# A four-layer conditioned transformer on one core: modulations computed with the condition as weights, and an MLP that may start before the last attention block ends

## The chip, the core and the metric

The kernel runs on one core of a Trainium2 chip. The core has five engines that work at the same time, each through its own list of instructions in order: TensorE (PE in the profile) multiplies matrices, VectorE (DVE), ScalarE (ACT) and GpSimd (POOL) work on elements, and SyncE (SP) here only issues DMAs. Engines wait for one another through semaphores. The metric is the time of one execution on the device, in microseconds.

## The reference

The input `x` has 16 samples of 256 tokens and 256 features. It passes through four layers, L0 to L3, and all of it is in 32-bit floats. L0, L2 and L3 have self-attention (16 heads of 16 features), cross-attention to a context of 77 tokens, and an MLP of width 1024. L1 has cross-attention alone. The layers' norms are shifted and scaled by vectors that come from the condition, one vector per sample:

```python
# L2; L0 and L1 are alike, and L3 takes c without the silu
c_proj = jax.nn.silu(c) @ W_mod + b_mod          # c is 16 x 256
shift_a, scale_a, gate_a, shift_m, scale_m, gate_m = jnp.split(c_proj, 6, axis=-1)
x_norm = modulate(_ln(x), shift_a, scale_a)      # t * (1 + sc[:, None]) + shift[:, None]
...
x_norm2 = modulate(_ln(x), shift_m, scale_m)
h = jax.nn.gelu(x_norm2 @ W_mlp1 + b_mlp1)
h = h @ W_mlp2 + b_mlp2
x = x + gate_m[:, None] * h
```

Ten such pairs of shift and scale are needed in the four layers. (L0 takes its condition without the silu too.) Attention uses an exponential for its softmax, the MLP a gelu; both are functions that ACT looks up in tables.

## The kernel before

**Blocks.** `x` stays in on-chip memory for the whole run (`x_sb`). The work is cut into blocks, one for each sample and each attention or MLP. `attention` (line 729 on) makes one attention block, `mlp` (line 1037 on) one MLP block. The stages follow each other as a, b (L0), c, d (L1 and L2), e, f (L3): a, c and e are attention, b, d and f are MLP. Within an attention stage the blocks of all samples are mixed, self-attention of one sample beside cross-attention of another.

**The planner.** The program's order is not that of the code. Each block adds tasks to a list (`od.add`): an engine, an assumed duration, the function that issues the instructions, the tasks it depends on, the buffers it takes, and a priority that grows from block to block. `Order.solve` then plays the list through with these durations. Whenever an engine is free it takes, of the tasks whose dependences and buffers are there, the one with the lowest priority (on TensorE), and two tasks that use different 32-row parts of TensorE's array are started as a pair (`rp`). The tasks are issued in the order that comes out, and every engine keeps to it on the chip, so an engine whose next instruction waits holds back all that stands behind it. A change in one assumed duration can move tasks anywhere after it. A pool of buffers is named by its tag; `b` are the eight PSUM banks that TensorE writes to, `kq` five large buffers that hold queries and keys, or weights, and `tmp` two buffers.

**One attention block.** A norm (DVE statistics at L460 and L461, POOL reciprocal root at L466 and L467, POOL scaling at L491) is turned by DVE (L519) and two DMAs (L524 out, L528 in), and ACT applies the modulation (L539). TensorE multiplies with the weights (L619, in 32-column parts; L628), in rotated blocks the result goes by DVE and POOL (L704) and is turned back by TensorE (L724). TensorE's scores for the maxima (L844, L856) go to DVE (L874, L878); the scores for the softmax (L937) to ACT's exponential (L949, L951); TensorE multiplies with the values (L960); DVE and POOL divide (L969, L976, L982, L986); `residual` multiplies with the output weights (L619 again) and adds to `x_sb`.

**One MLP block.** The same norm, then four tasks of TensorE with the first weights (L1059), each followed by a pair of gelus on ACT (L1064), then the second weights (L1010, in two halves). The weights (1 MB each) lie in two `kq` buffers.

**Barriers.** The task lists hold two kinds of wait between stages. `before` (all norms of the attention stage are done) holds the MLP's norms. `barrier` (all exponentials of the attention stage are done) holds the MLP's first product: `open_h` at line 1049 has it among its dependences, and nothing of L1059 can start before it. In the other direction, `attention` has a barrier of its own at its exponentials, which waits for all gelus of the MLP stage before. The gates' rows that an MLP block loads (`gate_tasks`) wait for `barrier` too.

**A modulation.** `modulation` (line 368 on) loads 512 columns of the weights (256 features by 512 columns, two rows of tiles `k`), and multiplies. The weights are TensorE's stationary side (`lhsT`), the condition, 16 columns, its moving side, so that the result stands with features on partitions, as ACT needs it at L539. These are eight multiplications at L382. DVE adds the bias (L387) and the 1 of the scale. The rows for the gates are computed the other way round, with the condition as the stationary side (L411). The modulations of L1 to L3 are placed beside MLP blocks of the stage before (`when`).

Of the kernel before, what the change touches and what calls it, by code (L numbers as in the profile page):

```python
# [58 lines left out]


class Task:
    __slots__ = ("eng", "dur", "run", "deps", "take", "prio", "rp", "left", "ready", "outs", "held", "start", "end", "no", "since", "kind", "more",
                 "lat", "first", "mb")


# [8 lines left out]
class Order:  # L74
# [3 lines left out]
    TURN = {"row": 0.2, "col": 0.13}  # L78
    PATIENCE = 2.0
    FAVOUR = 3.0  # L80
    PER_MB = 2.7
    def __init__(self, caps):
        self.caps, self.tasks = caps, []
# [14 lines left out]
        self.tasks.append(t)  # L98
        return t

    def solve(self):
        import heapq
        caps = self.caps
        loose = {k: list(range(n)) for k, n in caps.items()}
        free, waiting, events, result = {}, {}, [], []
        seq, n_done, now, mode, moved = 0, 0, 0.0, None, 0.0
        for t in self.tasks:
            if not t.left:
                waiting.setdefault(t.eng, []).append(t)

        def room(t, more=()):
            need = {}
            for h in list(t.take) + list(more):
                if h.no < 0:
                    need[h.tag] = need.get(h.tag, 0) + 1
            return all(len(loose[k]) >= n for k, n in need.items())

        def begin(ts):
            nonlocal seq, mode, moved
            dur = max(t.dur for t in ts) + sum(t.more for t in ts)  # L120
            if ts[0].eng == "PE":
                kind = "row" if ts[0].rp is not None else ts[0].kind
                dur += self.TURN.get(kind, 0.2) if kind != mode else 0.0
                mode = kind
            for t in ts:
                for h in t.take:
                    if h.no < 0:
                        h.no = loose[h.tag].pop(0)
                t.start, t.end = now, now + dur + t.lat
                if t.mb:  # L130
                    moved = max(now + dur, moved) + t.mb * self.PER_MB
                    t.end = moved + t.lat
                waiting[t.eng].remove(t)
                seq += 1
                heapq.heappush(events, (t.end, seq, t))
            if ts[0].eng != "NO":
                free[ts[0].eng] = now + dur
            result.append((now, len(result), ts))

        def choose(cand):  # L140

            lone = None
            for t in cand:
                if t.rp is None:
                    return [t]
                mates = [u for u in cand if u.rp == 1 - t.rp and room(t, u.take)]
                if mates:
                    return [t, min(mates, key=lambda u: (u.kind == t.kind, u.prio, u.no))]
                if lone is None:
                    lone = t  # L150
                    if t.since is None:
                        t.since = now
            if lone is not None and (now >= lone.since + self.PATIENCE - 1e-9 or not events):
                return [lone]
            return None

        while n_done < len(self.tasks):
            progress = True
            while progress:
                progress = False  # L160
                for eng in list(waiting):
                    if eng != "NO" and free.get(eng, 0.0) > now + 1e-9:
                        continue
                    cand = [t for t in waiting[eng] if t.ready <= now + 1e-9]
                    cand.sort(key=lambda t: (t.prio, t.no) if eng == "PE" else (not t.first, t.prio, t.no) if eng in ("SP", "NO") else
                              (not t.first, t.ready - self.FAVOUR * any(h.tag == "b" for h in t.held), t.prio, t.no))
                    cand = [t for t in cand if room(t)]
                    if cand:
                        ts = choose(cand) if eng == "PE" else [cand[0]]
                        if ts is not None:  # L170
                            begin(ts)
                            progress = True
            nxt = [e[0] for e in events[:1]]
            nxt += [t.ready for ts in waiting.values() for t in ts if t.ready > now + 1e-9]
            nxt += [t.since + self.PATIENCE for t in waiting.get("PE", ())
                    if t.since is not None and t.since + self.PATIENCE > now + 1e-9]
            assert nxt, "no step can start"
            now = min(nxt)
            while events and events[0][0] <= now + 1e-9:
                _, _, t = heapq.heappop(events)  # L180
                n_done += 1
# [13 lines left out]
def pixart_kernel(ctx: ExitStack, tc: tile.TileContext, x, cond_t, ctx_in, mask_c, mask_s, tables, vecs, rows,  # L195
# [32 lines left out]
    def psum(h, *dims):  # L228

        t = banks[h.no]  # L230
        return t.rearrange("p (a b) -> p a b", a=dims[0]) if dims else t
# [134 lines left out]
    gate_d, gate_t = {}, {}  # L366

    def modulation(name, src, col, shift_at, scale_at, c_t, bias, norm=None, gate=None, deps=(), prio=0, gprio=None):
        hw, hm, s = Hold("kq"), Hold("b"), {}
        m = mods[name] = const.tile([P, 4, B], F32, name=f"mod_{name}")  # L370

        def load():
# [1 line left out]
            nc.sync.dma_start(s["w"], src[:, :, col:col + 512])  # L374

        def mults():
            ps = psum(hm)
            s["ps"] = ps[:, 0:4 * B].rearrange("p (s b) -> p s b", b=B)
            for i, at in enumerate((shift_at, scale_at)):
                for c in range(NC):  # L380
                    for k in range(NC):
                        nc.tensor.matmul(s["ps"][:, 2 * i + c, :], lhsT=s["w"][:, k, at + c * P:at + (c + 1) * P],  # L382
                                         rhs=c_t[:, k, :], start=(k == 0), stop=(k == NC - 1))

        def take():
            v = vec[:, VOFF[bias]:VOFF[bias] + 4].unsqueeze(2).to_broadcast([P, 4, B])
# [4 lines left out]
                for c in range(NC):  # L391
                    nc.vector.tensor_scalar(m[:, 2 + c, :], m[:, 2 + c, :], 1.0, vcol(norm, c), ALU.add, ALU.mult)
        t0 = add("SP", ISSUE, load, deps=deps, take=[hw], prio=prio, mb=0.5, lat=2.0)
        t1 = add("PE", 2.0, mults, deps=[t0], take=[hm], use=[hw], prio=prio)
        mod_t[name] = add("DVE", 0.6, take, deps=[t1], use=[hm], prio=prio)
        if gate is None:
            return
# [639 lines left out]
    def mlp(b, name, wv, h_w, w_t, eps, mod, func, b1, pre_add, gate, prio, barrier, before):  # L1037
        s, nm = {}, f"{name}{b}"
        x_t = join([x_done[b], before], prio)
        xT_t, hx = norm_tasks(s, b, eps, mod, nm, prio, deps=[x_t])  # L1040
        if gate is not None:
            gate_tasks(s, b, gate, nm, prio, [barrier, xT_t])
        early_add(s, b, pre_add, prio)
        gel, he = [], Hold("ec")

        def open_h():
            for i in range(4):
                s["h", i] = buf(he)[:, i]
        t_h = add("NO", 0.0, open_h, deps=[xT_t, w_t["w1"], barrier], take=[he], prio=prio)
        for i in range(4):  # L1050
            hq, u = Hold("b"), {}

            def mm(i=i, u=u, hq=hq):
                ps = psum(hq)
                u["p"] = ps.rearrange("p (j n) -> p j n", j=2)
                for j in range(2):
                    f = 2 * i + j
                    for k in range(NC):
                        nc.tensor.matmul(u["p"][:, j, :], lhsT=wv["w1"][:, k, f * P:(f + 1) * P],  # L1059
                                         rhs=s["xT"][:, k, :], start=(k == 0), stop=(k == NC - 1))  # L1060

            def act(i=i, u=u):
                for j in range(2):
                    nc.scalar.activation(s["h", i][:, j, :], u["p"][:, j, :], func, bias=vcol(b1, 2 * i + j))  # L1064
            a = add("PE", 4 * MM, mm, deps=[t_h], take=[hq], use=[he, hx, *h_w], prio=prio)
            gel.append(add("ACT", 0.98, act, deps=[a], use=[hq, he], prio=prio))
        residual(s, b, [*gel, w_t["w2"]], lambda k, t: s["h", k // 2][:, k % 2, t * P:(t + 1) * P], lambda: wv["w2"], NF,
                 [he, *h_w], gate, nm, prio)
        return gel
# [311 lines left out]
```

## Time and profile before

Three runs took 2614.37, 2617.77 and 2619.29 us. A fourth execution was profiled.

| What | Value |
|---|---|
| Median of three runs | 2617.77 us |
| The profiled execution's own time | 2619.31 us |
| Its span, first instruction to last | 2617.4 us |
| Mean granted TensorE clock | 0.991 of full speed |
| TensorE instructions with L382 (modulations) | 160, in 21.4 us |
| ACT busy | 1284.3 us in 2559 instructions |
| ACT table loads | 6, of 1283 ns each |
| First gelu of the stages b, d, f | at 631.5, 1595.9, 2393.5 us |

A line such as `L382` is a line of the kernel. A multiplication in 32-bit floats stands in the trace as two instructions, a turn by TensorE as one. The waits name the engine that waited, the operation it waited for, the total in us, how often, and the longest. The granted clock is the share of TensorE's full clock; at half of it a matmul takes twice its time, and the profile still calls TensorE busy.

### The profile page before, as it was taken

Reading aid. Unit: us, or ns where it says so; the run is one execution under the profiler, and the core shown is the slowest. Engines: PE = TensorE matmul, PEld = TensorE weight load, DVE = VectorE, ACT = ScalarE, POOL = GpSimd, SP = SyncE. Lnnn points to the kernel's source line nnn. Section 1 sums busy time; section 2 is a strip of 40 time slices with the busy share of each in tenths; the row PEclk is TensorE's granted clock in tenths of the full one; section 3 lists DMA queues with packets and bytes.
Section 4 is the critical chain, followed back from the end, with each engine's and each line's share of the span. In section 5 each row is a group of like instructions: output and inputs, shape, how many; then the busy total and the mean of one; then the engine's idle time right before and its main releaser. Section 6 shows DMA issues by size and latency. Waiting matters only on the chain. (4 is left out here: it accounts for less than half of the span.)

```text
span 2617.4 us, 71563 instructions
## 1 busy us (share of the span) xinstructions
PE 2562.5 (98%) x29192; PEld 1677.9 (64%) x29192; DVE 1596.0 (61%) x4489; ACT 1284.3 (49%) x2559; POOL 1138.9 (44%) x1429
## 2 busy tenths in 40 slices
PE   8999999999999899999999999999999999998999
PEld 4555555556888656555556567888555555566888
DVE  6788886775130567777777784111878887885100
ACT  2555555564333456565556564232455555554322
POOL 5344434566552355333335566432233334557310
PEclk9999999999999899999999999999999999999999
DMA  5110111224221121111111123111100001121110
GB/s 173 31 32 26 35 33 40 69 79 136 69 78 53 40 70 51 57 52 40 40 41 46 55 79 106 60 61 41 36 28 28 28 28 38 46 77 57 57 57 29
DMA packets 159809, 144.08 MB, mean 55 GB/s; under 512 B 24648, under 2 KB 124216, under 8 KB 158712
## 3 DMA queue, kind: packets, MB, share of 16 engines
q1 hardware_dynamic: 159480, 139.51, 17.1%
q8 instruction: 229, 3.75, 0.6%
q14 instruction: 100, 0.82, 0.1%
HBM read 91.86 MB, written 47.61 MB: 53 GB/s over the span
## 5 line engine op out<-in xcount | busy, mean ns | idle before, releaser
L951 ACT ACTIVATE ec<-bank 128x512 f32<-128x512 f32 (+1 forms) x1152 | 611.6, 596 | 505.1 <-PE bank L844 300.2
L937 PE MATMUL bank<-kq 32*128 32x256 f32 (+1 forms) x5120 | 638.3, 395 | 4.9 <-ACT ec L949 2.7
L491 POOL TENSOR_SCALAR xn<-x_sb,mv,rstd 128x256 f32<-128x256 f32 x320 | 452.6, 1469 | 112.4 <-DVE y L519 101.3
L937 PEld LDWEIGHTS bank<-kq 32*128 32x128 f32 (+1 forms) x5120 | 360.3, 167 | 186.5 <-issue 96.7
L844 PE MATMUL bank<-kq 32*128 32x512 f32 x1536 | 446.8, 634 | 1.6 <-ACT ec L951 0.8
L874 DVE TENSOR_REDUCE mx<-bank 128x2 f32<-128x512 f32 x544 | 342.3, 680 | 59.3 <-PE bank L844 58.2
L1064 ACT ACTIVATE ec<-bank,vec 128x256 f32<-128x256 f32 x384 | 159.9, 467 | 403.1 <-PE bank L1059 365.5
L960 PE MATMUL bank<-ec,v 128*32 128x256 f32 (+1 forms) x5120 | 351.7, 385 | 5.2 <-ACT ec L951 2.9
L1059 PE MATMUL bank<-xT,kq 128*128 128x256 f32 x1536 | 344.1, 381 | 0.0
L1010 PE MATMUL bank<-kq,ec 128*128 128x256 f32 x1536 | 340.2, 379 | 0.0
L1059 PEld LDWEIGHTS bank<-xT,kq 128*128 128x128 f32 x1536 | 291.9, 191 | 42.1 <-issue 2.8
L1010 PEld LDWEIGHTS bank<-kq,ec 128*128 128x128 f32 x1536 | 291.2, 190 | 41.3 <-issue 2.1
L982 POOL TENSOR_TENSOR od<-ts,rec 128x128 f32<-128x128 f32 x448 | 170.9, 403 | 319.5 <-DVE rec L976 319.3
L519 DVE STREAM_TRANSPOSE y<-xn 128x512 f32<-128x512 f32 x158 | 110.6, 700 | 306.9 <-DMA yd<-y 255.2
L960 PEld LDWEIGHTS bank<-ec,v 128*32 128x32 f32 (+1 forms) x5120 | 156.4, 110 | 158.6 <-issue 39.4
L878 DVE TENSOR_REDUCE mx<-bank 128x4 f32<-128x308 f32 x512 | 211.6, 468 | 41.5 <-PE bank L937 30.0
L870 DVE CUSTOM_DVE_ANT_0 junk<-bank,ctx 128x256 f32<-128x256 f32 x448 | 189.0, 422 | 51.6 <-PE bank L844 22.1
L969 DVE STREAM_TRANSPOSE ts<-bank 128x512 f32<-128x512 f32 x224 | 157.8, 705 | 68.0 <-PE bank L960 57.9
L466 POOL TENSOR_SCALAR rstd<-mv 128x2 f32<-128x2 f32 x160 | 37.9, 237 | 352.8 <-DVE mv L461 281.3
L704 POOL TENSOR_TENSOR qk<-qk,rope 128x512 f32<-128x512 f32 (+1 forms) x96 | 113.7, 1185 | 175.5 <-DVE rope L699 118.7
L856 PE MATMUL bank<-kq 32*128 32x154 f32 x2048 | 166.4, 307 | 3.3 <-ACT ec L951 1.1
L844 PEld LDWEIGHTS bank<-kq 32*128 32x128 f32 x1536 | 136.6, 183 | 40.0 <-ACT ec L951 24.6
(162 smaller groups left out, 3255.9 us busy)
## 6 DMA issues: line engine op xcount, KB each, us to landing
yd<-y SPq DMA_DIRECT2D x158, 256.0 KB
xr<-yd SPq DMA_DIRECT2D x158, 256.0 KB
kq<-in_mod_dram SPq DMA_DIRECT2D x10, 512.0 KB
cin<-in_ctx_in_dram SPq DMA_DIRECT2D x36, 128.0 KB
x_sb<-in_x_dram SPq DMA_DIRECT2D x16, 256.0 KB
gb<-gate_g0m SPq DMA_DIRECT2D x16, 256.0 KB
gb<-gate_g2a SPq DMA_DIRECT2D x16, 256.0 KB
gb<-gate_g2m SPq DMA_DIRECT2D x16, 256.0 KB
```

The source lines that it names most:

```text
L491: nc.gpsimd.tensor_scalar(to, of, s["mv"][:, t, 0:1], s["rstd"][:, t:t + 1], ALU.subtract, ALU.mult)
L844: ls.append(lambda ps=ps, R=R, keys=keys: nc.tensor.matmul(ps.rearrange("p (s k) -> p s k", k=N), lhsT=s["qx"][R, 0, g, t * P:(t + 1) * P] ...
L856: ls.append(lambda ps=ps, R=R, keys=keys, tt=tt: nc.tensor.matmul(ps[:, 2 * tt * n:2 * (tt + 1) * n].rearrange("p (s k) -> p s k", k=n), l ...
L870: nc.vector.tensor_tensor_reduce(junk, u[i][:, i2 * N:(i2 + 1) * N], mb[:, t, :], -1.0, 3.0e38, ALU.add, ALU.min, m[:, i2, g, t:t + 1])
L874: nc.vector.tensor_reduce(m[:, :, g, t], u[i].rearrange("p (s k) -> p s k", k=N), AX.X, ALU.max, negate=True)
L878: nc.vector.tensor_reduce(m[:, :, g].rearrange("p s t -> p t s"), u[i][:, 0:4 * n].rearrange("p (t s k) -> p t s k", s=2, k=n), AX.X, ALU. ...
L937: (lambda ps=u[i], R=R, q=q: nc.tensor.matmul(ps[0:rows_n, q * N:(q + 1) * N], lhsT=s["kz"][R, q, g, kc * P:kc * P + rows_n], rhs=s["qx"][ ...
L951: nc.scalar.activation(e, u[i][0:rows_n], AF.Exp)
L960: nc.tensor.matmul(u5["p"][32 * r:32 * r + 32, 1 - q, :], lhsT=s["v"][0:rows_n, kc, 8 * g + 2 * r + 1 - q, :], rhs=s["e", g, kc, r][0:rows ...
L982: nc.gpsimd.tensor_tensor(ov[:, :, HD * i:HD * i + HD], ts[:, i, :, HD * i:HD * i + HD], rec[:, i, :].unsqueeze(2).to_broadcast([P, N // 3 ...
L1010: nc.tensor.matmul(u["p"][:, t, :], lhsT=lhsT(k, t), rhs=w()[:, k, :], start=(k == 0), stop=(k == nk - 1))
L1059: nc.tensor.matmul(u["p"][:, j, :], lhsT=wv["w1"][:, k, f * P:(f + 1) * P], rhs=s["xT"][:, k, :], start=(k == 0), stop=(k == NC - 1))
```

## The change

`modulation` now takes the condition as TensorE's stationary side (16 columns) and moves the 512 columns of the weights past it, in two multiplications. The result has samples on partitions, so ACT copies it out of PSUM to a `tmp` buffer, and TensorE turns it in four pieces of 16 by 128 to the old layout in a second PSUM bank. DVE goes on as before. One planner task of TensorE with the assumed duration 2.0 becomes three, of 0.95 on TensorE, 0.6 on ACT and 0.4 on TensorE.

In `mlp`, `open_h` loses `barrier` from its dependences. `before` stays on the norms, and `barrier` stays on the loads of the gates' rows. Exponentials of the last attention blocks and gelus of the first MLP blocks may now alternate on ACT.

`Order.solve` gets an argument `seed` and a field `rank` that takes the place of the priority on TensorE: the priority plus a random number that counts only where the seed is above 0. The call passes none.

```diff
@@ class Order @@
     FAVOUR = 3.0
+    CHANCE = 4.0
...
-    def solve(self):
+    def solve(self, seed=0):
+
         import heapq
+        import random
+        rng = random.Random(seed)
         caps = self.caps
+        for t in self.tasks:
+            t.rank, t.left, t.ready, t.since = t.prio + self.CHANCE * rng.random() * (seed > 0), len(t.deps), 0.0, None
+            for h in t.held:
+                h.no, h.users = -1, 0
+        for t in self.tasks:
+            for h in t.held:
+                h.users += 1
...
-                    return [t, min(mates, key=lambda u: (u.kind == t.kind, u.prio, u.no))]
+                    return [t, min(mates, key=lambda u: (u.kind == t.kind, u.rank, u.no))]
...
-                    cand.sort(key=lambda t: (t.prio, t.no) if eng == "PE" else (not t.first, t.prio, t.no) if eng in ("SP", "NO") else
+                    cand.sort(key=lambda t: (t.rank, t.no) if eng == "PE" else (not t.first, t.prio, t.no) if eng in ("SP", "NO") else
@@ modulation @@
-        hw, hm, s = Hold("kq"), Hold("b"), {}
+        hw, hr_, hc, hm, s = Hold("kq"), Hold("b"), Hold("tmp"), Hold("b"), {}
...
         def mults():
-            ps = psum(hm)
-            s["ps"] = ps[:, 0:4 * B].rearrange("p (s b) -> p s b", b=B)
+            for k in range(NC):
+                nc.tensor.matmul(psum(hr_)[0:B], lhsT=c_t[:, k, :], rhs=s["w"][:, k, :], start=(k == 0),
+                                 stop=(k == NC - 1))
+
+        def copy():
+            s["r"] = buf(hc).rearrange("b t d -> b (t d)")
+            nc.scalar.copy(s["r"][0:B], psum(hr_)[0:B])
+
+        def turn():
+            s["ps"] = psum(hm)[:, 0:4 * B].rearrange("p (s b) -> p s b", b=B)
             for i, at in enumerate((shift_at, scale_at)):
                 for c in range(NC):
-                    for k in range(NC):
-                        nc.tensor.matmul(s["ps"][:, 2 * i + c, :], lhsT=s["w"][:, k, at + c * P:at + (c + 1) * P],
-                                         rhs=c_t[:, k, :], start=(k == 0), stop=(k == NC - 1))
+                    nc.tensor.transpose(s["ps"][:, 2 * i + c, :], s["r"][0:B, at + c * P:at + (c + 1) * P],
+                                        ident[0:B, 0:B])
...
-        t1 = add("PE", 2.0, mults, deps=[t0], take=[hm], use=[hw], prio=prio)
+        t1 = add("PE", 0.95, mults, deps=[t0], take=[hr_], use=[hw], prio=prio)
+        t1 = add("ACT", 0.6, copy, deps=[t1], take=[hc], use=[hr_], prio=prio)
+        t1 = add("PE", 0.4, turn, deps=[t1], take=[hm], use=[hc], prio=prio)
@@ mlp @@
-        t_h = add("NO", 0.0, open_h, deps=[xT_t, w_t["w1"], barrier], take=[he], prio=prio)
+        t_h = add("NO", 0.0, open_h, deps=[xT_t, w_t["w1"]], take=[he], prio=prio)
```

More of the change, by code (lines that the diff above doesn't have):

```diff
@@ L61 @@
 class Task:
-    __slots__ = ("eng", "dur", "run", "deps", "take", "prio", "rp", "left", "ready", "outs", "held", "start", "end", "no", "since", "kind", "more",
+    __slots__ = ("eng", "dur", "run", "deps", "take", "prio", "rp", "left", "ready", "outs", "held", "start", "end", "no", "since", "kind", "more", "rank",
                  "lat", "first", "mb")
```

## The prediction

> **What bounds the kernel now.** I read the page's busy line first, then busy time by stretches, then TensorE's waits, then the timeline at the places that the change touches.
>
> ```profile
> span 2617.4 us, 71563 instructions
> PE 2562.5 (98%) x29192; PEld 1677.9 (64%) x29192; DVE 1596.0 (61%) x4489; ACT 1284.3 (49%) x2559; POOL 1138.9 (44%) x1429
> ```
>
> TensorE is the bound: 98% busy, the others at 61% or less. Only two things can therefore move the time: work added to or taken from TensorE, and the 55 us in which it idles, with what idling does to its clock. In the next answer the columns are length, PE busy (instructions), granted clock, DMA share, GB/s. The stretches are the change from attention to MLP in the first layer (two), in the third (two) and in the fourth, and last a stretch of MLP alone.
>
> ```profile
> 578.00:597.00 19.00, 16.93 (x228) 0.91 0.34 108
> 597.00:632.00 35.00, 30.25 (x319) 0.85 0.29 88
> 1550.00:1578.00 28.00, 26.23 (x391) 1.00 0.37 119
> 1578.00:1593.00 15.00, 13.62 (x196) 1.00 0.40 138
> 2357.00:2388.00 31.00, 22.16 (x290) 0.89 0.20 66
> 2388.00:2440.00 52.00, 52.00 (x295) 1.00 0.15 51
> ```
>
> The MLP has no gaps and the full clock; the changes do not. Idle is 2.07 + 4.75 us in the first, 1.77 + 1.38 in the third layer, 8.84 in the fourth. The clock takes more: 0.09 x 19 = 1.7 and 0.15 x 35 = 5.25 us, none, and 0.11 x 31 = 3.4 us. So the three cost 13.8, 3.2 and 12.2 us, 29 us in all. That is what an earlier MLP can fill. The largest waits:
>
> ```profile
> PE bank L619 <- ACT xT L539: 8.3, 2, 7.8
> PE bank L724 <- POOL qk L704: 7.9, 5, 5.4
> ```
>
> The 7.8 us lie at 872, from MLP back to attention, which the barrier in question does not touch. The 5.4 us lie in the fourth layer's change: TensorE's turn of the last query waits for POOL's addition, queued behind a scaling of an MLP block (2.8 us).
>
> **Part 1, the modulations.** Ten times, eight multiplications (128-column weights, 16 moving columns) become two (16-column weights, 512 moving columns), a copy by ACT and four turns. TensorE's timeline has the old form, and L411, which is the new form with 256 columns:
>
> ```profile
> 923.59 1.04 PE L411 MATMUL bank<-kq,scondT 128*16 128x256 f32 x4
> 924.56 0.60 PE L436 MATMUL bank<-row,ident 16*16 16x256 f32 x2
> ...
> 931.71 1.96 PE L382 MATMUL bank<-scondT,kq 128*128 128x16 f32 x16
> ```
>
> Each matmul is two records. The old form holds TensorE 1.85 us (16 records; the end of the last overlaps what follows). The next task after L411 starts 924.56 - 923.59 = 0.97 us later, of which about 0.11 is the change of tile mode (below): two matmuls of 256 columns take 0.86. Two of 512 columns take 1.73, with a mode change 1.83. The larger moving side eats what the fewer weight loads save: nothing is gained here. The four turns come on top. Not shown at 16 columns, they are bounded by the nearest row, L724 (320 turns of 128 columns, 47.7 us: 0.149 each, 0.6 for four), and below by L382's records, 16 weight loads of the same width in 1.85 (0.116 each, 0.46 for four); I take 0.5, since the moving side is as small as L382's. Against 1.85 stand 1.83 + 0.5: +0.48 us each, **+4.7 us** for ten (ends 3 and 7).
>
> The copy: L1024's 128x512 copy takes 0.58, so 5.8 us of ACT, 49% busy. It hides behind its gelus, and TensorE's wait for it behind the one to four tasks that stand between product and turn (an MLP product is 1.73, half of a second MLP product 3.45). Only two have nothing between: the first of all, in TensorE's start-up waits, where the turns of xn queue behind it but POOL delivers xn last at 12.56 (+0.2 us), and "1k", inside the 7.8 us idle at 872. Without cover each costs 0.6 + 0.3, and the MLP product queued behind the turn, then its gelus, come later by that. A modulation now takes two of the eight PSUM banks and one of two `tmp` buffers, for some 3 us each. The DMAs stay as they are: one 512 KB load each.
>
> **Part 2, the barrier.** The first MLP products no longer wait for the last exponential. Nothing is removed from any engine; the planner now deals first-layer products between the last attention blocks. The program's order, which can be listed without a run, shows: ACT changes tables 18 times for 6, four more in each of the three changes; score tasks 633 in pairs and 14 alone, for 635 and 10; changes of tile mode on TensorE 1098, for 1057, twenty of the 41 beside the new turns. Half of an attention block's output product takes 0.864 with its own kind after it and 0.977 before another: 0.11 per change, 21 x 0.11 = 2.3. Summing for both orders each task's median step among the same neighbours gives, the turns aside, +0.8 us, since cheaper neighbours make up for some; **+0.8** (ends 0 and 4).
>
> What the table loads cost is read from ACT's groups:
>
> ```profile
> L1064 ACT ACT_TABLE_LOAD x3 | 3.8, 1283 | 13.5 <-PE bank L1059 13.5
> L951 ACT ACT_TABLE_LOAD x2 | 2.6, 1283 | 0.0
> ```
>
> 1.28 each, 12 x 1.28 = 15.4 us of ACT, and they count only where TensorE outruns them. The Trainium skill (ScalarE: Activation LUTs, What ACT_TABLE_LOAD costs) adds a drain of about 1.38 to a switch, 2.66 in all. In the trace the load of 899.50 starts 10 ns after the operation before and the exponential 10 ns after it: no drain shows. By the rule the six switches that TensorE waits on below would cost 1.38 more each, and the sum would end at 2620; I take the row.
>
> The walk, with TensorE's steps from the trace (pair of scores 1.03, values 0.98, first-layer MLP task 1.73, attention output 0.88 a half, MLP output 3.45 a half) and ACT's (exponential 0.60, pair of gelus 0.84, xT 1.09):
> - Third layer: scores, two MLP tasks (3.46), values. ACT needs 1.28 + 4 x 0.60 + sync = 3.9: wait 0.5. Then scores, half an MLP output, which needs the fourth gelu pair, behind a load, a pair, xT: wait 2.0. Then 0.2. Total 2.7, with 1 us more for waits that the order of DVE and DMA makes: 3.7 where 3.2 was: +0.5.
> - First layer: the same waits come to 1.7. Before them TensorE stands at the output of the fourth-last block: POOL has five reciprocal roots (0.95), a scaling (2.83), a residual and two divisions before it, 9.4 us, and DVE turns the result back (0.4), against 6.9 of TensorE work: 2.9. With 1.7 of clock for such a gap, as at 578, and 1 us of small ones: 7.3 for 13.8, **-6.5**.
> - Fourth layer: the addition now stands before the second scaling, not after it: the 5.4 goes. The scores behind the turn wait for ACT's query (1.2), the first MLP task for its turned input (2: two DMAs and xT against three TensorE tasks), the interleaving 1.6, clock 1.5: 6.3 for 12.2, **-5.9**.
>
> What is late next is the second scaling on POOL, needed only two blocks later. The weight loads on SP (1 MB each, 6 to 8 us at the 137 to 184 GB/s around them) stand 25 to 30 us before their first use.
>
> The clock weighs here. The Trainium skill (TensorE: Matmul & The Clock Gate, What's actually happening) lets the clock fall after an idle window of about 3.4 us. In 597 to 632 no wait is over 1.1 us, and the mean clock is 0.85. By the rule that loss would come from elsewhere and stay: the first layer would gain 2, and the sum be 2617. I go by the row.
>
> The planner's new argument stays at 0, so its rank is the old priority: no effect.
>
> **The sum**: 4.7 + 0.8 + 0.2 + 0.5 - 6.5 - 5.9 = -6.2, and with 0.4 us back for waits that a new order makes elsewhere, -5.8. The profiled execution took 2619.31 (span 2617.4 and 1.9 around it), 1.5 above the median 2617.77: it gives 2613.5, the median **2612**.
>
> **Rivals.** 0.2% (5.2 us) is about what a measurement of this kernel can tell from no change.
> - *The waits move, they don't go* (0.20). For: POOL is 85% busy in 597 to 632 and its queue, not the barrier, sets the output waits. Against: the 5.4 us have a visible place in an order that changes. The first and fourth layer give 3 each: 4.7 + 0.8 - 6 = 2617, 2615 to 2621.
> - *The table loads come onto the path* (0.20). For: where TensorE has 3.46 us between scores and values, ACT is already short. It decides as soon as ACT enters such a place over 1 us late: then every load is TensorE's wait, 15.4 us, and the clock stays low. Less the 5 that the walk counts: 2612 + 10 + 4 of clock = 2626. Against: half an MLP output (3.45) mostly stands behind.
> - *The modulations do become cheaper* (0.12): were a 512-column record to cost what a 256-column one does, the product would take 0.95, -0.4 each with the turns: 2603. Against it stands L411.
> - *The barrier was not what held the MLP*: excluded, the order moves.
>
> Forecast 0.48, itself 2607 to 2617, about half of it beyond 0.2%. Faster 0.26 + 0.12 = 0.38; same 0.22 + 0.16 = 0.38; slower 0.04 + 0.20 = 0.24. Range 2603 to 2626, from the third rival's time to the second's: about half of each lies beyond, 0.16 in all. The ends of the modulations (-1.7, +2.3) and modes (-0.8, +3.2) lie inside it, around the forecast.
>
> **What would show it.** The product's four records spanning about 1.8 us, the turns 0.5; 18 table loads; the idle of the fourth change under 5 us, its 5.4 us wait gone; the clock of the first at 0.93 or more. I am wrong if waits on ACT's exponentials exceed 8 us in the changes, or if a new wait of over 3 us stands in the attention stages, where only the planner's order has moved.

## The result, and the profile after

The changed kernel takes 2612.16 us (median of 19 runs, 2606.89 to 2615.12) against 2617.77 of the kernel before (median, 2611.22 to 2625.25 in the same sitting): the ratio is 0.9974, 95% interval 0.9965 to 0.9982, so it is faster by 0.26%. The forecast was 2612. The number was met, but the experiments below show that two of the steps under it were wrong, in opposite directions.

The profiled execution took 2614.68 us, with a span of 2612.9. First the page's busy line, then busy time by stretches, the same six as in the prediction (length, PE busy, granted clock, DMA share, GB/s), then TensorE's waits (total, times, longest).

```profile
span 2612.9 us, 71467 instructions
PE 2557.2 (98%) x29112; PEld 1662.3 (64%) x29112; DVE 1595.6 (61%) x4489; ACT 1301.9 (50%) x2581; POOL 1136.2 (43%) x1429
```

```profile
578.00:597.00 19.00, 19.00 (x312) 1.00 0.53 166
597.00:632.00 35.00, 28.17 (x262) 0.95 0.30 93
1550.00:1578.00 28.00, 24.73 (x333) 0.94 0.37 123
1578.00:1593.00 15.00, 14.26 (x124) 1.00 0.27 89
2357.00:2388.00 31.00, 27.70 (x234) 0.83 0.24 79
2388.00:2440.00 52.00, 51.75 (x340) 1.00 0.14 47
```

```profile
PE bank L648 <- DVE ctx L1245: 7.3, 2, 5.0
PE bank L639 <- DVE oT L1006: 7.1, 4, 4.8
PE bank L744 <- POOL qk L724: 4.0, 4, 1.7
```

Worked as in the prediction, idle and clock loss of the first layer's change are now 6.8 + 1.75 = 8.6 us (13.8 before), of the third's 4.0 + 1.7 = 5.7 (3.2), of the fourth's 3.3 + 5.3 = 8.6 (12.2). The 5.4 us wait of the fourth change is gone (1.7 is left). In the first, the wait at the output of the fourth-last block is there, 4.8 us. The 7.8 us idle near 872 has a new name, the scaled context, and nearly its old size.

The groups of ScalarE with the table loads, and TensorE's and ScalarE's instructions of the modulations (duration min/median/max in ns, first to last start):

```profile
L1084 ACT ACT_TABLE_LOAD x9 | 11.5, 1283 | 4.8 <-PE bank L1079 4.7
L971 ACT ACT_TABLE_LOAD x6 | 7.7, 1283 | 2.1 <-PE bank L957 2.0
L969 ACT ACT_TABLE_LOAD x2 | 2.6, 1283 | 0.0
```

```profile
L389 PE MATMUL bank<-kq,condT x24: 589/592/1057, 7.1 to 1875.4; 128*16 128x512 f32 x24
```

```profile
L400 PE MATMUL bank<-ident,tmp x40: 176/208/236, 11.1 to 1877.0; 16*128 16x16 f32 x40
```

A product spans 1.82 us from its first record to the next task, as forecast (1.83; the old one spans 1.70 beside MLP tasks and up to 1.89 elsewhere). Four turns hold TensorE 0.35, not 0.5. So a modulation costs TensorE about 0.3 us more than before, and ten cost 3, where the prediction had 4.7.

To see where the time went, the span is cut at moments that both kernels share (the end of the same block's residual) and each piece is split into TensorE's idle time, the loss to the clock (half of the time that the trace's clock record shows at half speed), and the rest, which is work at full clock. What half speed does can be read in the kernel before: the same 32 records of the output product (L619) take 1.93 us at 495.70 and 3.64 us at 503.99, where the clock is at half.

| piece, us before | length | idle | clock loss | work |
|---|---|---|---|---|
| first layer's attention, to 451 | +2.5 | +2.7 | +1.7 | -1.9 |
| its end, the change, MLP, to 735 | -4.2 | +0.6 | -8.5 | +3.7 |
| MLP, to 812 | -1.5 | -0.6 | 0 | -0.9 |
| back to attention, to 1238 | -3.4 | +1.0 | -3.4 | -0.9 |
| the third layer's change, to 1657 | +3.3 | +0.5 | +1.7 | +1.0 |
| MLP, fourth layer's attention, to 2208 | -1.4 | -3.3 | 0 | +1.9 |
| the fourth layer's change, to 2451 | +0.2 | -0.3 | +3.4 | -3.0 |

In sum the clock gave 5.1 us, idle time took 0.6, and the work stayed the same. The clock's record begins only 16.5 us into the span before, and 10.0 after, so the 1.7 and -1.9 of the first row are not to be read: at 17 us the two kernels are level. From there on the clock gave 6.8 us, idle time took 0.5 and the work 1.9. Either way the gain is a gain of clock. And the record of the clock names two places that the prediction had not looked at: before, it is at half speed from 501.2 for 6.8 us and from 910.8 for 10.2 us, 8.5 us of loss, each time within 3 us of the start of a modulation's product (499.9 and 907.9). After, nothing is there.

### The profile page after: what moved, and what is told of

The parts are those of the page before. It is cut to its first block, busy times and chain, and to the rows that moved or that the text cites. A ratio compares the mean times of both kernels' runs of the same rounds, so it can differ in the third digit from the quotient of the medians.

```text
span 2612.9 us, 71467 instructions
## 1 busy us (share of the span) xinstructions
PE 2557.2 (98%) x29112; PEld 1662.3 (64%) x29112; DVE 1595.6 (61%) x4489; ACT 1301.9 (50%) x2581; POOL 1136.2 (43%) x1429
## 3 DMA queue, kind: packets, MB, share of 16 engines
q1 hardware_dynamic: 159480, 139.51, 17.2%
## 5 line engine op out<-in xcount | busy, mean ns | idle before, releaser
L957 PE MATMUL bank<-kq 32*128 32x256 f32 (+1 forms) x5120 | 626.6, 395 | 0.7 <-ACT ec L971 0.5
L864 PE MATMUL bank<-kq 32*128 32x512 f32 x1536 | 438.2, 634 | 1.4 <-ACT ec L971 0.8
L980 PE MATMUL bank<-ec,v 128*32 128x256 f32 (+1 forms) x5120 | 346.4, 383 | 3.6 <-ACT ec L971 2.1
L1051 POOL TENSOR_TENSOR x_sb<-x_sb,tmp 128x512 f32<-128x512 f32 x80 | 101.9, 1274 | 135.6 <-DVE tmp L1046 134.2
```

The source lines that it names most:

```text
L864: ls.append(lambda ps=ps, R=R, keys=keys: nc.tensor.matmul(ps.rearrange("p (s k) -> p s k", k=N), lhsT=s["qx"][R, 0, g, t * P:(t + 1) * P] ...
L957: (lambda ps=u[i], R=R, q=q: nc.tensor.matmul(ps[0:rows_n, q * N:(q + 1) * N], lhsT=s["kz"][R, q, g, kc * P:kc * P + rows_n], rhs=s["qx"][ ...
L980: nc.tensor.matmul(u5["p"][32 * r:32 * r + 32, 1 - q, :], lhsT=s["v"][0:rows_n, kc, 8 * g + 2 * r + 1 - q, :], rhs=s["e", g, kc, r][0:rows ...
```

## The experiments

Microseconds from a ratio below are (ratio - 1) x 2618. The kernel before was measured again beside each group.

**The parts alone, the table loads, the order.** The barrier alone, in the kernel before:

```diff
-        t_h = add("NO", 0.0, open_h, deps=[xT_t, w_t["w1"], barrier], take=[he], prio=prio)
+        t_h = add("NO", 0.0, open_h, deps=[xT_t, w_t["w1"]], take=[he], prio=prio)
```

> The kernel before with the barrier taken off the MLP's first product, and the old modulations. Theory (the barrier brings the gain, the modulations cost): without their +3 us (2.16 us each in the trace after, 1.85 before) this is faster than the full change, 2606 to 2611. Rival (the gain is the luck of one order among many): anywhere from 2607 to 2623, unrelated to the parts. Second rival (the modulations bring the gain): 2615 to 2620. It changes tables 22 times where the full change does 18 times.

Measured: 2607.05 us, ratio 0.9948 (0.9928 to 0.9968), -13.6 us. The modulations alone (the same line put back in the changed kernel):

```diff
-        t_h = add("NO", 0.0, open_h, deps=[xT_t, w_t["w1"]], take=[he], prio=prio)
+        t_h = add("NO", 0.0, open_h, deps=[xT_t, w_t["w1"], barrier], take=[he], prio=prio)
```

> The changed kernel with the barrier put back on the MLP's first product: the new modulations alone, 6 table loads. Theory: 10 x 0.3 us more of TensorE than before, 2618 to 2623. Rival (luck of the order): anywhere from 2607 to 2623. Second rival (the modulations bring the gain): 2610 to 2614.

Measured: 2614.18 us, ratio 0.9979 (0.9967 to 0.9990), -5.5 us. This is a miss: the modulations, priced at +4.7, bring a gain when they come alone. The changed kernel without the table loads of the gelus (a plain addition of the bias stands in for the gelu, so the MLP's nonlinearity is left out):

```diff
-                    nc.scalar.activation(s["h", i][:, j, :], u["p"][:, j, :], func, bias=vcol(b1, 2 * i + j))
+                    nc.scalar.activation(s["h", i][:, j, :], u["p"][:, j, :], AF.Identity, bias=vcol(b1, 2 * i + j))
```

> The changed kernel in the same order, with an identity in place of every gelu, so that the nonlinearity of the MLPs is left out and ACT loads one table in all instead of 18. If the loads are mostly hidden behind TensorE, as the walk had it (4 to 5 us of waits behind them): 2607 to 2611. If every load between attention and MLP is TensorE's wait: 17 x 1.28 = 22 us less, 2590. If none counts: 2612.

Measured: 2607.2 us, ratio 0.9955 (0.9939 to 0.9971). 17 loads less, 21.8 us of ScalarE, give 0.19%, 5 us, with about as much either way, since the two intervals overlap: some quarter is on the path, which agrees with the walk (5 of 15.4 us) but doesn't prove it. The same tasks in another order, from the planner's own argument:

```diff
-    for ts in od.solve():
+    for ts in od.solve(seed=1):
```

> The changed kernel with the planner's random numbers switched on (seed 1): the same tasks, durations and dependences, another order of TensorE's tasks. If orders of equal work agree within the measurement: 2610 to 2615. If the order alone moves the time as much as the change did (5.6 us): 2616 to 2630, or under 2607.

Measured: 2623.12 us, ratio 1.0014 (1.0 to 1.0028). The same instructions in another order are 10.5 us slower (1.0014 against 0.9974), more than the whole change brought. So a difference of two kernels whose order differs says little about the edit.

The barrier alone is ahead of the kernel before by 4.7 us at the end of the first MLP and by 22.8 at 1543: it gains 18 us where the MLP hands back to attention, which the barrier does not touch. There the modulation "1k" waits for its weights, which wait for one of five buffers. The load of "1k" on the DMA timeline of the kernel before:

```profile
865.70 0.58 SPq L374 DMA_DIRECT2D kq<-in_mod_dram  x1
```

and of the barrier-only kernel:

```profile
675.11 0.57 SPq L374 DMA_DIRECT2D kq<-in_mod_dram  x1
```

**"1k" early.** If that is the cause, allowing this one modulation earlier must do the same with no other edit:

```diff
-    modulation("1k", mod1, 512, 256, 0, scondT, "m1k", **when(3))
+    modulation("1k", mod1, 512, 256, 0, scondT, "m1k", **when(1))
```

> The kernel before, with one call altered: the modulation 1k may be issued one stage earlier, beside the other modulations of block 1, so that its weights are loaded long before the second change from MLP to attention (near 870 us) and its product doesn't wait there. Barrier and modulations are those of the kernel before, so the table loads stay 6. Theory A (the barrier-only run won at that change because its 1k weights came in at 675 us and not at 866 us, and not through the barrier): this kernel wins nearly all of that without touching the barrier, 10 to 16 us, 2602 to 2608 us; no TensorE gap above 3 us within 865 to 885 us. Theory B (the barrier-only run won because MLP blocks could begin early): nothing of it here, 2614 to 2620 us, ratio 0.999 to 1.001. Theory C (each planned order falls by luck within some 10 us): 2607 to 2625 us, and the gap at 870 us may go without the time following.

Measured: 2603.28 us, ratio 0.9953 (0.9940 to 0.9965), -12.3 us. Busy time in the stretch 855 to 925, of the kernel before:

```profile
855.00:925.00 70.00, 60.49 (x644) 0.85 0.16 50
```

and with "1k" early:

```profile
855.00:925.00 70.00, 67.15 (x837) 1.00 0.22 65
```

Idle falls from 9.5 to 2.9 us and the clock is full: 60.49 x 0.85 = 51.4 us of full-clock work become 67.2. Theory A holds, without barrier or new modulations. The same edit with the new modulations and the barrier, and in the whole changed kernel:

> The changed kernel with its barrier put back (6 table loads), and the modulation 1k issued early as in the run beside it: the new modulations alone, on a base without the stall at 870 us. Theory A: the new form costs what its steps in the trace say, some +0.3 us for each of ten, so +2 to +4 us against the early-1k kernel with the old form: 2604 to 2612 us. Theory that the new form itself brings the gain: 3 to 5 us below that kernel. Luck of the order: anything within 10 us of it.

> The changed kernel with the modulation 1k issued early: new modulations, barrier off, 18 table loads. Theory A (the stall at 870 us cost both kernels alike): 8 to 14 us below the changed kernel, 2598 to 2605 us, the fastest of these or level with the early-1k kernel of the old form. If the barrier's freedom is worth about 1 us, as the difference between the changed kernel and its modulations alone says, then it lies within 3 us of the run with barrier and early 1k. Luck of the order: 2602 to 2618 us.

Measured: 2613.78 us, ratio 0.9995 (0.9986 to 1.0004), and 2609.83 us, ratio 0.9977 (0.9966 to 0.9988). Both are misses: the first is 11 us slower than "1k" early with the old form, where 2 to 4 had been expected, and the second is level with the changed kernel, where 8 to 14 us less had been expected. Both win the place (at 1500 us they are 15 us ahead of the kernel before, by the count of TensorE's instructions without the modulations, and the early-1k kernel 16), and both give it back later: some 8 us go at the third layer's change, where no line was altered, and about 1 with the old form. Two kernels in the stretch 1545 to 1620, "1k" early with the old form and with the new:

```profile
1545.00:1620.00 75.00, 71.44 (x681) 1.00 0.34 109
```

```profile
1545.00:1620.00 75.00, 69.45 (x691) 0.93 0.34 112
```

So a local gain can be given back some 650 us further on. That the order does it, and not the new form in itself, was not separated here. The last of this group, again with "1k" early and the old form, lets the products of the first MLP block of a stage begin early, but not its gelus, so that no table loads are added (6 in all):

```diff
-        t_h = add("NO", 0.0, open_h, deps=[xT_t, w_t["w1"], barrier], take=[he], prio=prio)
+        t_h = add("NO", 0.0, open_h, deps=[xT_t, w_t["w1"], barrier if b else None], take=[he], prio=prio)
...
-            gel.append(add("ACT", 0.98, act, deps=[a], use=[hq, he], prio=prio))
+            gel.append(add("ACT", 0.98, act, deps=[a, barrier], use=[hq, he], prio=prio))
```

> The kernel before with 1k issued early, and the barrier moved: the first product of the first MLP block may run beside the last attention blocks, but its gelus wait for the barrier as before, so no table loads come in on top of the 6. Theory: the cover at the three changes without the loads, which cost about 5 us of 22 when they are taken away whole: 2 to 6 us below the early-1k kernel that keeps the barrier, 2598 to 2604 us. If the barrier is worth nothing but its loads' price, it is level with it within 2 us. If banks that hold the early product starve the attention blocks: 2 us or more slower.

Measured: 2631.14 us, ratio 1.0053 (1.0039 to 1.0067), the slowest of all. The third layer's change, first with "1k" early alone, then here:

```profile
1545.00:1625.00 80.00, 76.44 (x704) 1.00 0.36 114
```

```profile
1545.00:1625.00 80.00, 74.15 (x730) 0.89 0.32 105
```

The clock is at half speed for 17 us there. Products that wait for their gelus hold PSUM banks, so that fewer are left to the attention blocks; that this is the cause was argued, not shown.

**One order, both forms.** To take the order out, three kernels use the changed kernel's list of steps as it stands. In the first the product's step does the eight small multiplications of the old form, ScalarE's copy goes straight to the modulation's tile (DVE then adds the bias in place), and the turning step is empty:

```diff
-            for k in range(NC):
-                nc.tensor.matmul(psum(hr_)[0:B], lhsT=c_t[:, k, :], rhs=s["w"][:, k, :], start=(k == 0),
-                                 stop=(k == NC - 1))
+            s["ps"] = psum(hr_)[:, 0:4 * B].rearrange("p (s b) -> p s b", b=B)
+            for i, at in enumerate((shift_at, scale_at)):
+                for c in range(NC):
+                    for k in range(NC):
+                        nc.tensor.matmul(s["ps"][:, 2 * i + c, :], lhsT=s["w"][:, k, at + c * P:at + (c + 1) * P],
+                                         rhs=c_t[:, k, :], start=(k == 0), stop=(k == NC - 1))
...
-            nc.scalar.copy(s["r"][0:B], psum(hr_)[0:B])
+            nc.scalar.copy(m, s["ps"])
```

> The changed kernel's own order of steps, barrier off and all, with the ten modulations computed in the old form at the place of the new product: eight small products into 64 columns of the bank, ScalarE copies these straight to the modulation's tile, and the step that turned them issues nothing. So the form of the modulation changes and no other step moves. Theory A (the new form costs about 0.3 us each beside its turns, and two turn waits of 0.7 us): 3 to 5 us below the changed kernel, 2607 to 2610 us. Theory B (the new form is what brings the gain, by lighter work on TensorE): 2 to 5 us above it, 2614 to 2617 us. Theory C (the form is of no consequence, all is order): within 1.5 us of the changed kernel.

Measured: 2624.28 us, ratio 1.0018 (1.0007 to 1.0029). In the same order the old form is 0.44%, 11.5 us, slower than the new, where theory A had expected it to be 3 to 5 us faster. In the second, "1k" and the two steps that scale the context with it are moved beside "1q", with a buffer of their own for the weights:

```diff
+    q, k = chain["1q"][0], chain["1k"][0]
...
+    steps = [ts for ts in steps if ts[0] not in [*k, *m1]]
+    at = [steps.index([t]) for t in q]
+    for i, t in sorted([(at[0] + 1, k[0]), (at[2] + 2, k[1]), (at[3] + 2, k[2]), (at[3] + 6, k[3]), (at[4] + 6, k[4]),
+                        (at[4] + 130, m1[0]), (at[4] + 136, m1[1])], key=lambda u: -u[0]):
+        steps.insert(i, [t])
```

> The changed kernel's own order of steps, with the chain of modulation 1k alone moved: its weights go into a buffer of their own (the two rotary buffers, which lie idle there), loaded right after those of 1q near 660 us; its product, copy, turn and the two multiply-adds that scale the context follow 1q's steps. All other steps keep their order, so luck of the order is out. Theory A (the restart near 870 us stalls for this chain): the TensorE gaps of 5.0 and 2.3 us at 870 to 876 us go and the half clock after them; 8 to 13 us below the changed kernel, 2599 to 2604 us, and nothing given back later. Theory B (the block behind it waits for something else as well, and the gap moves): 0 to 5 us below, 2607 to 2612 us, with a new wait within 865 to 890 us.

Measured: 2614.42 us, ratio 0.9979 (0.9968 to 0.9990): no gain. TensorE's idle of 7.3 us in two pieces from 869.6 goes, and one of 9.3 us stands at 872, before the first scores, which need DVE's half of the key. ScalarE's timeline of this kernel shows why (start, duration, and in brackets the idle before and what ended it):

```profile
879.47 1.09 ACT L562 ACTIVATE xT<-xr,mod_1q 128x256 f32<-128x256 f32 x2 [8.63 <-DMA xr<-yd]
880.47 0.70 ACT L676 ACTIVATE kq<-bank,kb_bk,par 128x77 f32<-128x77 f32 x2
```

The key's step (L676) stands in ScalarE's queue behind another block's turned input (L562), which waits 8.6 us for a normalisation on POOL and a DMA. The late weights of "1k" were one of two chains of about the same length. The edit of `when` worked because the planner, told that "1k" is early, also dealt the queues anew. Both edits in this order:

> Both edits of the two runs beside it, the order of steps else that of the changed kernel: old form of the modulations, chain of 1k early. If the two effects are real and separate they add: 11 to 17 us below the changed kernel, 2595 to 2601 us, the fastest of all runs. If they don't add (one hides the other), level with the run with 1k early, within 1.5 us.

Measured: 2624.76 us, ratio 1.0020 (1.0008 to 1.0031). The difference of the forms is there again, 10.7 us (1.0020 against 0.9979).

What the difference consists of, by the four profiled executions (clock loss without the tail after TensorE's end):

| order | old form less new | span | clock loss | idle | work |
|---|---|---|---|---|---|
| changed kernel's | first of these less changed kernel | +9.7 | +6.8 | +5.6 | -2.7 |
| the same, "1k" moved | third less second | +11.0 | +10.2 | +4.4 | -3.6 |

The old form is the lighter by 2.7 to 3.6 us of work, near the 0.3 us each read from the records. From 17 us on, where the clock's record covers all four alike, the rows read +8.5, +5.8, -5.3 and +10.2, +4.8, -5.4, so the last column is good to a few microseconds only. In both readings the old form loses more to the clock than it saves in work. The granted clock of every run says it too, not the profiled ones alone: the mean over 12 runs is 0.9898 with the old form, over 19 runs 0.9933 with the new, so the clock's part of the time is 26.7 and 17.5 us. With "1k" moved it is 24.9 and 17.2.

**What lets the clock fall.** In the old form 16 columns are sent through behind each load of 128. The last kernel is the one with the old form in the changed kernel's order, and sends the same 16 columns eight times over, with nothing else altered:

```diff
-                        nc.tensor.matmul(s["ps"][:, 2 * i + c, :], lhsT=s["w"][:, k, at + c * P:at + (c + 1) * P],
-                                         rhs=c_t[:, k, :], start=(k == 0), stop=(k == NC - 1))
+                        nc.tensor.matmul(wide[:, 2 * i + c, :].rearrange("p (r b) -> p r b", b=B),
+                                         lhsT=s["w"][:, k, at + c * P:at + (c + 1) * P],
+                                         rhs=c_t[:, k, :].unsqueeze(1).to_broadcast([P, 8, B]), start=(k == 0),
+                                         stop=(k == NC - 1))
```

> The run with the old form in the changed kernel's order, and one thing altered: each of the eight small products of a modulation sends the 16 columns of the condition through eight times over (128 moving columns for 16; the copies land in columns that nobody reads). Same order, same loads, same waits, TensorE only busier within the same steps. In the runs with the old form the granted clock fell to half right behind some of these products (at 506 us for 3.4 us and at 909 us for 10.2 us in the run with the old form in this order; 0.91 and 0.80 in the windows 495 to 515 and 900 to 925 us), and in none of those with the new form outside the change at 870 us. Theory A (the sparse products, 16 moving columns behind each load of 128, let the clock fall): with 128 columns both stretches go, the clock in the two windows is 1.00, and the time falls by 5 to 9 us against that run, to 2615 to 2620 us, ratio to the kernel before 0.998 to 1.000. Theory B (the clock falls there for the waits around the products, whatever their columns): both stretches stay, 2622 to 2628 us, ratio 1.001 to 1.004. Theory C (the old form costs its time through longer waits, not the clock): the stretches go but the time moves by less than 3 us.

Measured: 2615.69 us, ratio 1.0007 (0.9999 to 1.0016). Busy time around the modulations near 501 and 907 us (columns as above), of the kernel before, of the changed kernel, of the old form in the changed order, and of the same with wide products:

```profile
495.00:515.00 20.00, 19.43 (x244) 0.83 0.25 69
900.00:925.00 25.00, 24.53 (x273) 0.80 0.20 61
```

```profile
495.00:515.00 20.00, 19.81 (x297) 1.00 0.39 103
900.00:925.00 25.00, 24.78 (x340) 1.00 0.25 68
```

```profile
495.00:515.00 20.00, 19.21 (x281) 0.91 0.28 83
900.00:925.00 25.00, 23.16 (x273) 0.80 0.16 47
```

```profile
495.00:515.00 20.00, 19.08 (x284) 1.00 0.34 104
900.00:925.00 25.00, 23.64 (x328) 1.00 0.27 77
```

With wide products both stretches at half clock are gone. In the first, TensorE idles as much as with the small products (19.08 and 19.21 of 20 us busy), so there the moving columns decide. The second is not as clean. With the small products the clock falls there half a microsecond after the product has begun, behind a wait of 1.6 us:

```profile
908.63 3.09 PE L392 MATMUL bank<-scondT,kq 128*128 128x16 f32 x16 [1.61 <-DVE st L478]
```

The wide product waits 1.15 us in the same place, so part of that difference may be the wait.

The other traces say more. Within a trace all stretches at half speed begin and end on one grid of 3.41 us, so a trace can be cut into such windows. Six kernels have the old form (the kernel before, the barrier alone, "1k" early, the gelus that wait, and two in the changed order). At full clock, 34 of their windows hold 1.6 us or more of its products. In 26 of these TensorE has one product and no idle time: no fall of the clock follows. In six it has one product and also idles for 0.07 to 1.46 us: a fall follows each time. In two it has two products back to back and no idle time, and a fall follows both times. (Windows that hold less of a product go both ways. That before the fall at 501.2 has 1.25 us of product and 0.40 of idle time.) This is one of the two, in the kernel with "1k" early (first the stretch around it, with the fall at 664.3 for 3.4 us):

```profile
655.00:675.00 20.00, 20.00 (x102) 0.91 0.32 104
659.72 3.64 PE L382 MATMUL bank<-scondT,kq 128*128 128x16 f32 x32
```

In the seven kernels with the new form 40 windows hold as much of a product, ten of them with 0.04 to 1.37 us of idle time; in the wide form there are six, one of them with 0.80. No fall follows any of these. So one product of 16 moving columns does not bring the clock down alone, and a short wait beside a product of 128 or 512 columns does not either. The small product together with a short wait does, and so do two small products without any wait. (Elsewhere the clock also falls behind windows without a modulation, with 0.5 to 3.4 us of idle time in them. What the other tasks contribute there is not shown.)

The profiled span falls by 10.0 us from the small products to the wide ones, 8.5 of them clock. The size is less certain than the mechanism: by the ratios it is 0.11%, 2.9 us with some 3.6 us either way, since this group ran on another chip, where the kernel before also had more clock (0.9931 for 0.9920). Taking the kernel before as the measure on each chip, the clock lost over it falls from 5.7 us to 1.5. Theory A holds for the clock and for the median (2615 to 2620); its ratio (0.998 to 1.000) is missed, and theory C's bound of 3 us cannot be excluded. By the ratios some 8.6 us between the wide old form (1.0007) and the new (0.9974) stay without an explanation; the profiled spans of the two are equal (2612.6 and 2612.9).

## Why the prediction was right, and where it was not

The median met the forecast, and no rival's time came true. The first rival's mechanism did: the waits moved and did not go, for TensorE idles 55.7 us in all, where it idled 54.9. The signs that the prediction had named all came (product 1.8 us, 18 loads, 3.3 us of idle in the fourth change, a clock of 1.00 and 0.95 in the first), and they didn't show that two steps were wrong. Step by step:

- *TensorE is the bound, and only its work, its idle time and its clock count*: held as far as it was tried (21.8 us taken from ScalarE moved the time by some 5). That the tables add up in these three shows nothing, since work is what is left over.
- *The modulations, +4.7*: the durations were nearly right (product 1.82 for 1.83, turns 0.35 for 0.5, so 3 for 4.7), the step was wrong in sign. "The larger moving side eats what the fewer weight loads save: nothing is gained here" counted TensorE's time and not what the instructions do to its clock. In one order the new form is 10.7 to 11.5 us faster. The prediction looked for clock loss only in the three changes; the same view at 495 to 515 and 900 to 925 us would have shown 0.83 and 0.80 beside two modulations, with hardly any idle time.
- *The price of copies, +0.2, and the waits for them*: two turn waits of 0.7 us, at the first modulation and at "1k", the two places named. The first layer's attention lost 2.5 us in all.
- *Other work, +0.8 (ends 0 and 4)*: missed. The old form in the changed order has 2535.8 us of full-clock work, the kernel before 2538.7: the new order is 2.9 us cheaper.
- *First layer, 7.3 for 13.8*: 8.6. The wait at the output of the fourth-last block came where it was forecast, for the reason given, with 4.8 us for 2.9. The clock's part fell from 6.95 to 1.75, as the row, not the rule, had suggested. Idle time stayed (6.8 us before and after), where 5.6 had been forecast. But the kernel with the barrier kept gains as much up to the steady MLP (4.6 us in that piece of the table, against 4.2), and 3.4 of the 8.5 us of clock in that piece belong to the modulation at 499.9: the barrier is not shown to be the cause.
- *Third layer, 3.7 for 3.2*: 5.7 in the same stretches, and over the whole piece +3.3. Too small by 2 to 3.
- *Fourth layer, 6.3 for 12.2*: 8.6 in the stretch, since the 5.4 us wait went but the clock fell to 0.83 where 1.5 us of loss were allowed for. Over the whole piece nothing was gained (+0.2), and the barrier alone loses 7 us there (22.9 us ahead of the kernel before, then 15.7).
- *Table loads, hidden but for some 5 us*: agrees (5 us, not clear of noise), and no drain after a load shows: in every kernel with gelus some loads are followed by ScalarE's next instruction within 11 to 12 ns.
- *+0.4 for waits that a new order makes elsewhere*: this was the weakest term. Order alone moves this kernel by 10 us and more.

So the sum was right by errors that cancel, and that it met the median to a microsecond is luck. In the one order that can be compared, going from the kernel before to the old form in the changed order (barrier off) costs +4.7 us by the ratios, where -10.7 had been forecast for all but the modulations, and going on to the new form gives -11.5, where +4.9 had been forecast. Even this split is one of several: through the barrier alone it reads -13.6 and then +6.8, through the modulations alone -5.5 and then -1.3. What a part of this change is worth depends on the order that the planner makes of it, and only the total is a fact.

Two of the kernels beat both: "1k" early (2603.28 us, 0.9953) and the barrier alone (2607.05 us, 0.9948), level with each other within their intervals. The first is one argument of one call.

## What to carry to other kernels

Before an edit that changes the shape of TensorE's instructions is priced by their durations, read the granted clock around them: here many loads with few moving columns cost more in clock behind them than in time, wherever a short wait stood beside them. Where a planner orders the work, first measure how far another order of the same tasks moves the time, and test a cause with the order held fixed. A stall that is removed by an earlier load may stand again behind the next chain of the same length, so list all chains that end at the same place. Name signs that would tell a wrong step from a right one, and not only signs that the new timing is there.

## What the runs showed of the hardware

- TensorE's clock fell to half behind products of 16 moving columns while TensorE was 97 to 98% busy (495 to 515 and 900 to 925 us in the kernel before), and stayed at full speed with 128 or 512 columns in the same places. One such product without idle time was never followed by a fall (26 windows), one with 0.07 us or more of idle time always was (six windows), and so were two back to back with TensorE 100% busy (two windows). The stretches at half speed last 3.4, 6.8, 10.2 or 13.7 us, multiples of the window that the Trainium skill names (TensorE: Matmul & The Clock Gate, What's actually happening, about 3.4 us). That page speaks of idle windows; here a window without any idle time was enough.
- The clock also goes with most of the scatter from run to run. In four groups of runs of the kernel before, on four chips (17 to 29 runs each), the granted clock lies between 0.989 and 0.995 and the time between 2609.3 and 2627.3 us; the two have a correlation of -0.87 to -0.96, at 1.7 to 2.5 us for each 0.001 of clock.
- Four turns of 16 columns took 0.35 us, 176 to 236 ns each by the records, which overlap.
